# A decoder layer's prologue: first scores by halves of the keys, chunk 1 between the first steps, other load order, idle matmuls

## The chip, the cores and the metric

The kernel runs on one core of one Trainium2 chip. The metric is the time of one execution in device microseconds (us), taken as the median over runs; lower is better. A core has five engines that work at the same time, each through its own instructions in order, and that wait for each other by semaphores: TensorE (PE, matrix products; its weight loads are listed apart as PEld), VectorE (DVE), ScalarE (ACT), GpSimd (POOL) and SyncE (SP), which here only issues transfers (DMAs). ACT issues some DMAs as well: such an issue stands in ACT's instruction order, and the transfer itself runs on the core's DMA engines. TensorE writes into PSUM, which has eight banks of 128 x 512 floats; DVE and ACT read results from there.

## The reference

One pre-norm decoder layer on x of shape (2, 1024, 256): self-attention, cross-attention to a context of 77 tokens, and a mixture of experts. All data are float32. The change touches only the beginning of the self-attention:

```python
x = x + _L0_attn_ref(_layernorm(x), Wq, Wk, Wv, rel_table, gamma, beta)
x = x + _L0_xattn_ref(_layernorm(x), ctx, ctx, mask, ...)
x = x + _L0_ffn_ref(_layernorm(x), ...)          # top 2 of 8 experts

def _L0_attn_ref(x, ...):                        # 16 heads of 16 channels
    q, k, v = (split_heads(x @ W) for W in (Wq, Wk, Wv))
    attn = softmax(einsum('bhqd,bhkd->bhqk', q, k) * e ** -0.5)
    attn = attn + rel_table[rel_index].reshape(h, s, s)[None]
    out = layernorm(merge_heads(einsum('bhqk,bhkd->bhqd', attn, v)), eps=1e-3)
    return out * gamma + beta
```

## The kernel before

The 2048 tokens lie in `xs` as 16 tiles of 128 rows; four tiles make a *chunk* (512 tokens), so chunks 0 and 1 are batch 0, and 2 and 3 are batch 1. The work of a chunk before attention is a chain of small helpers:

- `load_x(c)` (L98) loads the chunk from HBM by SP. `load_rows` (L105) loads a weight matrix, by ACT for Wk and Wq and by SP for Wv.
- `measure(c)` (L159, L160): mean and variance of each token, two DVE instructions a tile. `deviation(c)` (L136, L137): the variance plus epsilon on DVE, then to the power of -0.5 on POOL, whose second operand is the constant tile `nhalf`.
- `scale_tokens(0)` (L316) normalises chunk 0 on DVE. For other chunks `offsets(c)` (L172, DVE) and `scale(c)` (L183, four ACT instructions) do it.
- `turned(c, kc, copy)` (L193, L196): four transposes on TensorE into one PSUM bank, then one copy into `xnT`, by DVE or by ACT. There are two such halves `kc` of 128 channels.
- `project(w, name, j)` (L495): K or Q of 512 tokens for eight heads, two matmuls. Q is copied by ACT (L505). K is written twice by DVE (L510), once for each of two groups of heads, as `kT0` and `kT1`.
- `values(c, u)` (L333, L340): V of two tiles, four matmuls and an ACT copy into `vaug`. `clear(kt)` (L296, L297) fills the rest of `vaug` on POOL, `clear_rest` other tiles.

Wk and Wq lie in HBM in another order of heads than the projections need, so ACT rearranges them first, by four copies each (L279), out of `wkraw` and `wqraw`.

Attention is one stream of 128 steps (`for n in range(steps + 1)`), eight steps for each of 16 *halves* (a batch, a group of four heads, 512 queries). In step n, `stream_a` (L525) computes four score tiles of 128 queries by 512 keys, one for each head, and DVE takes the maximum of each row (L532). Two steps make one tile of 128 queries, since there are 1024 keys. Eight steps give the maxima of a half. `find_shift` (L540), `shift_queries` (L551, L554: four transposes into the tile `pm`, then one DVE instruction) turn them into an extra channel of the queries. Ten steps behind (`LAG = 10`), `stream_b` (L571) computes the scores again with keys in rows, already shifted; ACT takes their exponentials (L579), and `times_v` (L588) multiplies by V.

The order on TensorE, DVE, ACT and POOL is the order in which the program is written (`manual_schedule`); SP's instructions are ordered by the framework. `between` is a table of jobs that are written ahead of step n. In the kernel before, chunks 0 and 1 are measured, scaled and turned, and K of batch 0's first eight heads is projected for both, before step 0; the values of chunks 0 and 1, and chunks 2 and 3, follow in steps 0 to 8, the context's keys and values in steps 7 to 9. The loads are written at the head, from L245 on; the ACT ones (Wk, Wq) are the first instructions of ACT, ahead of its table load.

Of the kernel before, what the change touches and what calls it, by code (L numbers as in the profile page):

```python
# [11 lines left out]
ALU = mybir.AluOpType  # L12
AX = mybir.AxisListType

P = 128
# [25 lines left out]
def decoder_kernel(  # L41
# [55 lines left out]
    def load_x(c):  # L97
        nc.sync.dma_start(  # L98
            out=xs[:, 4 * c : 4 * c + 4, :],
            in_=xf[512 * c : 512 * c + 512, :].rearrange("(t p) d -> p t d", p=P),  # L100
        )
# [60 lines left out]
    def deviation(c, eps=1e-5):  # L162

        tokens[c] = norm_scale(moments[c][1], 4, eps)
# [78 lines left out]
    make_identity(nc, ident)  # L243
    nc.gpsimd.memset(nhalf, -0.5)
    load_x(0)  # L245
    for name, src in (("wk", a_wk), ("wq", a_wq)):
        raws[name] = load_rows(src, f"{name}raw", D, fst)
    load_x(1)
# [19 lines left out]
    nc.vector.tensor_reduce(  # L268
        hsel, ident.rearrange("p (a j r) -> p j a r", a=2, j=4), AX.XY, ALU.add
    )  # L270
    nc.scalar.mul(hsel, hsel, 0.25)
    for name, raw in raws.items():
        c0 = {"wk": 2048, "wq": 2560}[name]
        w = scrap[:, c0 : c0 + 512].rearrange(
# [17 lines left out]
    def clear(kt):  # L292

        part = vaug[:, kt : kt + 2]
        for k in range(2):
            nc.gpsimd.memset(part[:, k, :, DH:, :], 0.0)  # L296
            nc.gpsimd.memset(part[:, k, :, DH, :], 1.0)  # L297
# [188 lines left out]
    units = {}  # L486
    outs = {}

    def project(w, name, j):

        b, G = w // 2, w % 2
        cols = slice(512 * j, 512 * j + 512)
        pp = one("pp")
        for kc in range(2):
            nc.tensor.matmul(  # L495
                pp,
                lhsT=wqk[name][:, kc, P * G : P * G + P],
                rhs=xnT[:, kc, b * S + 512 * j : b * S + 512 * j + 512],
                start=(kc == 0),
                stop=(kc == 1),  # L500
            )
        if name == "wq":
            if j == 0:
                units[w, "q"] = scrap[:, 3584 + S * (w % 2) : 3584 + S * (w % 2) + S]
            nc.scalar.copy(units[w, "q"][:, cols], pp)  # L505
            return
        for i in range(2):
            if j == 0:
                units[w, "k", i] = at2.tile([P, S], F32, tag=f"kT{i}", name=f"kT{i}_{w}")
            nc.vector.tensor_scalar(  # L510
                units[w, "k", i][:, cols], pp, own[i][:, 0:1], extra[i][:, 0:1], ALU.mult, ALU.add
            )

    pieces = [("wk", 0), ("wq", 0), ("wk", 1), ("wq", 1)]
    largest = {}

    def stream_a(n, hh):
        h, r = n // 8, n % 8
        b, g, qb = halves[h]
        if h not in largest:  # L520
            largest[h] = at2.tile([P, 4, 4, 2], F32, tag="mx", name=f"mx{h}", bufs=3)
        qt, kh = r // 2, r % 2
        s = one("sA")
        r0, q0 = 32 * hh, 512 * qb + P * qt
        nc.tensor.matmul(  # L525
# [359 lines left out]
    def shared(c, u):  # L885

        psh = one("psh").rearrange("p (t f) -> p t f", f=D)
        for t in range(2):
# [12 lines left out]
    turns = [("a", 0), ("b", 1), ("a", 2), ("b", 3), ("b", 0), ("a", 1), ("b", 2), ("a", 3)]  # L901


    between = {
        0: [lambda: values(0, 0), lambda: measure(2)],
        1: [lambda: values(0, 1), lambda: deviation(2), lambda: clear(0)],
        2: [lambda: values(1, 0), lambda: project(0, "wq", 1), lambda: offsets(2), lambda: clear(2)],
        3: [lambda: values(1, 1), lambda: scale(2), lambda: measure(3), lambda: clear(4)],
        4: [
            lambda: turned(2, 0, by_act), lambda: turned(2, 1, by_act), lambda: deviation(3),  # L910
            lambda: clear(6), rest_of_loads,
        ],
        5: [lambda: values(2, 0), lambda: offsets(3), lambda: scale(3), clear_rest],
        6: [lambda: values(2, 1), lambda: turned(3, 0, by_act), lambda: turned(3, 1, by_act)],
        7: [lambda: values(3, 0), context_turn, lambda: context_keys(0)],
        8: [lambda: values(3, 1), lambda: context_keys(1), mask_bias],
# [11 lines left out]
    between.update({40 + 4 * c: [lambda c=c: add_rows(c, beta_a)] for c in range(4)})  # L928
    measure(0)
    deviation(0)  # L930
    measure(1)
    deviation(1)
    scale_tokens(0)
    turned(0, 0, by_dve)
    turned(0, 1, by_act)
    offsets(1)
    scale(1)
    project(0, "wk", 0)
    project(0, "wq", 0)
    turned(1, 0, by_dve)  # L940
    turned(1, 1, by_act)
    project(0, "wk", 1)

    def settle(c, n):

        key = "o", c
# [631 lines left out]
```

## Time and profile before

| | |
|---|---|
| median of 3 runs (lowest, highest) | 1005.02 us (1004.63, 1005.73) |
| the profiled execution | 1004.62 us, span 1002.9 us |
| mean granted TensorE clock | 0.956 |
| attention's stream of steps | from 24 us (first scores) to about 510 us |
| cross-attention and routing | to about 670 us |
| mixture of experts | to about 956 us, then the last sums and norms |
| first token load landed, DVE starts on it | 6.04 us |
| first instruction of TensorE | 11.24 us |
| first exponential of the stream | 60.13 us |

The span reaches from the first instruction of the program to its last; the time of the execution holds 1.7 us more. In a line of the timeline the first number is the start in us from the span's start, the second the length, then the engine, the source line, the operation, output and inputs, shapes and the number of instructions merged; in brackets stands the engine's idle time before it and what ended that. A float32 matrix product is recorded as two rows of TensorE, a transpose as one. In a line of the table of stretches, the first pair is the stretch, then come its length, the busy time of PE, PEld, DVE, ACT and POOL (with counts), the granted clock, the busy share of the DMA engines and the GB/s that they moved.

### The profile page before, as it was taken

The numbers are of one execution on the slowest core, as the hardware profiler recorded it, in microseconds if no ns is written. First come the engines' busy times: TensorE is split into PE (matmuls) and PEld (weight loads), VectorE is DVE, ScalarE is ACT, GpSimd is POOL, SyncE is SP. The second block draws the span as 40 slices with busy tenths as digits, with TensorE's granted clock in tenths as the row PEclk, the third lists the DMA queues.
The fourth block names the chain that finished last, engine by engine and source line by source line (L and its number), as shares of the span: only waits on it lengthen the run. The fifth ranks groups of instructions, "written<-read, shape, count | busy, mean of one in ns | idle before, by whom it ended". The sixth has DMA issues, their size and how long they took to land.

```text
span 1002.9 us, 15898 instructions
## 1 busy us (share of the span) xinstructions
PE 894.6 (89%) x5948; PEld 516.9 (52%) x5948; DVE 594.9 (59%) x1185; ACT 536.1 (53%) x1064; POOL 403.9 (40%) x336
## 2 busy tenths in 40 slices
PE   5999999999999999999946999979999999998900
PEld 2543433333333333333314667767788788887800
DVE  4876658877897787987589998760110110110057
ACT  3457667777887786887844777313322222233301
POOL 1533223553335544343466887023444421222125
PEclk9999999999999999999977999998999999998955
DMA  8200000000000000000000000146645645799152
GB/s 177 50 1 1 2 2 1 2 1 1 1 1 1 1 2 1 1 1 2 1 1 18 1 22 23 42 133 230 196 163 189 207 155 174 256 318 318 65 173 84
DMA packets 65143, 75.63 MB, mean 75 GB/s; under 512 B 17947, under 2 KB 57016, under 8 KB 65056
## 3 DMA queue, kind: packets, MB, share of 16 engines
q1 hardware_dynamic: 59040, 63.09, 19.9%
q0 software_dynamic: 3360, 8.79, 2.3%
q10 hardware_dynamic: 2656, 2.62, 0.8%
q8 instruction: 50, 0.82, 0.3%
q14 instruction: 37, 0.30, 0.1%
HBM read 66.10 MB, written 8.78 MB: 75 GB/s over the span
## 4 chain that ended last, share of the span: by engine, by line
PE 53%; DVE 14%; DMA 13%; issue 11%; POOL 6%; ACT 2%; POOLq 0%; ACTq 0%; DVEq 0%; SPq 0%
PE sA L525 15%; PE av L588 12%; DMA pairs<-y,to_row 11%; PE sB L571 11%; PE pp L495 3%; POOL pairs L1452 2%; PE pv L333 2%; DVE scrap L1516 2%; PE pb L387 1%; DVE cm L676 1%; PE ph L1422 1%; POOL xg L1396 1%; DVE cs L688 1%; PE pq L640 1%; DVE scrap L672 1%
## 5 line engine op out<-in xcount | busy, mean ns | idle before, releaser
L532 DVE TENSOR_REDUCE mx<-sA 128x1 f32<-128x512 f32 x512 | 317.5, 683 | 71.5 <-PE sB L571 63.8
L579 ACT ACTIVATE pt<-sB 128x512 f32<-128x512 f32 x512 | 264.6, 603 | 79.8 <-PE sB L571 79.6
L525 PE MATMUL sA<-kT,scrap 32*128 32x512 f32 x1024 | 259.2, 619 | 0.0
L601 POOL TENSOR_TENSOR avs<-avs,part 128x512 f32<-128x512 f32 x112 | 142.1, 1268 | 269.9 <-ACT part L600 264.6
L571 PE MATMUL sB<-qB,kT 32*128 32x512 f32 x1024 | 248.5, 616 | 0.0
L1429 ACT ACTIVATE hT<-ph,b1s 128x256 f32<-128x256 f32 (+1 forms) x184 | 77.8, 424 | 186.5 <-PE ph L1422 184.4
L525 PEld LDWEIGHTS sA<-kT,scrap 32*128 32x128 f32 x1024 | 101.5, 183 | 87.8 <-ACT pt L579 52.3
L1441 PE MATMUL po<-w,hT 128*128 128x256 f32 x560 | 139.2, 387 | 6.5 <-DVE y L1448 5.2
L1422 PE MATMUL ph<-xgT,w 128*128 128x256 f32 (+1 forms) x736 | 139.6, 336 | 2.0 <-ACT hT L1429 2.0
L588 PE MATMUL av<-pt,vaug 128*32 128x512 f32 x1024 | 137.4, 605 | 1.7 <-DVE mx L532 1.7
L1422 PEld LDWEIGHTS ph<-xgT,w 128*128 128x128 f32 x736 | 117.5, 193 | 26.7 <-ACT hT L1429 11.3
L1448 DVE TENSOR_TENSOR y<-po,b 128x512 f32<-128x512 f32 (+1 forms) x23 | 13.0, 564 | 187.1 <-PE po L1441 180.4
L571 PEld LDWEIGHTS sB<-qB,kT 32*128 32x128 f32 x1024 | 97.7, 183 | 38.4 <-issue 30.1
L1441 PEld LDWEIGHTS po<-w,hT 128*128 128x128 f32 x560 | 101.5, 192 | 21.3 <-DVE y L1448 8.3
L1452 POOL DMA_INDIRECT pairs<-y,to_row x35 | 35.5, 1016 | 123.9 <-DMA pairs<-y,to_row 82.5
L1396 POOL DMA_INDIRECT xg<-xnd,from_row x35 | 34.2, 976 | 100.0 <-PE px L1412 61.9
L588 PEld LDWEIGHTS av<-pt,vaug 128*32 128x32 f32 x1024 | 21.0, 109 | 98.8 <-DVE mx L532 85.3
L600 ACT COPY part<-av 128x512 f32<-128x512 f32 x108 | 65.6, 608 | 8.1 <-PE av L588 7.9
L137 POOL TENSOR_TENSOR rstd<-rstd,nhalf 128x4 f32<-128x4 f32 x20 | 21.7, 1086 | 68.3 <-DVE rstd L136 68.2
L193 PE MATMUL pxT<-ident,xn 128*128 128x128 f32 x96 | 18.2, 309 | 28.8 <-ACT xn L183 17.4
L495 PE MATMUL pp<-xnT,scrap 128*128 128x512 f32 x64 | 33.3, 648 | 0.4 <-DVE xnT L196 0.3
L705 ACT COPY PT<-ppT 77x512 f32<-77x512 f32 x64 | 32.4, 588 | 2.0 <-DVE xs L1052 1.0
(239 smaller groups left out, 958.3 us busy)
## 6 DMA issues: line engine op xcount, KB each, us to landing
w<-in_L_ffn_W_dram SPq DMA_DIRECT2D x46, 1024.0 KB, 7.4
b<-in_L_ffn_b_dram SPq DMA_DIRECT2D x23, 128.0 KB, 6.6
xs<-in_x_dram SPq DMA_DIRECT2D x4, 512.0 KB, 8.2
xnd<-xn SPq DMA_DIRECT2D x4, 512.0 KB, 2.9
w<-pairs SPq DMA_DIRECT2D x4, 512.0 KB, 9.4
w<-pairs ACTq DMA_DIRECT2D x4, 512.0 KB, 7.4
out_dram<-scrap SPq DMA_DIRECT2D x4, 512.0 KB, 2.9
mk<-in_mask_BxSxS_ik_dram SPq DMA_DIRECT2D x1, 616.0 KB, 6.0
```

What stands on the lines that cost most here:

```text
L495: nc.tensor.matmul(pp, lhsT=wqk[name][:, kc, P * G : P * G + P], rhs=xnT[:, kc, b * S + 512 * j : b * S + 512 * j + 512], start=(kc == 0), ...
L525: nc.tensor.matmul(s, lhsT=units[h // 4, "q"][r0 : r0 + 32, q0 : q0 + P], rhs=units[h // 4, "k", g % 2][r0 : r0 + 32, 512 * kh : 512 * kh ...
L532: nc.vector.tensor_reduce(largest[h][:, qt, hh : hh + 1, kh], s, AX.X, ALU.max)
L571: nc.tensor.matmul(s, lhsT=units[h // 4, "k", g % 2][r0 : r0 + 32, kt * P : (kt + 1) * P], rhs=shifted[h][r0 : r0 + 32, :], start=True, st ...
L579: nc.scalar.activation(powers[m, hh], s, AF.Exp, scale=1.0 / 16.0)
L588: nc.tensor.matmul(av[32 * hh : 32 * hh + 32, :], lhsT=vaug[:, kt, 4 * g + hh, :, b], rhs=powers.pop((m, hh)), start=True, stop=True,)
L600: copy(part, av)
L601: nc.gpsimd.tensor_tensor(sums[h], sums[h], part, ALU.add)
L1422: nc.tensor.matmul(ph[:, hc % group, :], lhsT=w1[:, kc, hc * P : (hc + 1) * P], rhs=xgT[:, kc, :], start=(kc == 0), stop=(kc == 1),)
L1429: hidden[i] = nc.scalar.activation(hT[:, hc, :], ph[:, hc % group, :], AF.Gelu, bias=b1s[:, i, hc : hc + 1])
L1441: nc.tensor.matmul(po[:, s, :], lhsT=hT[:, hc, s * P : (s + 1) * P], rhs=w2[:, hc, :], start=(hc == 0), stop=(hc == NH - 1),)
L1452: nc.gpsimd.indirect_dma_start(out=pairs[:, :], out_offset=bass.IndirectOffsetOnAxis(ap=to_row[:, k : k + 1], axis=0), in_=y[:, s, :], in_ ...
```

## The change

1. **Loads.** An ACT instruction that multiplies one column of `nhalf` by 1.0 is written ahead of the loads of Wk and Wq; it waits for POOL's fill of `nhalf`, and it brings ACT's table load with it. The scaling of `hsel` by 0.25 goes from ACT to DVE.
2. **Idle matmuls.** 22 products of the identity matrix with itself go to a PSUM bank that nobody reads, as the first work of TensorE.
3. **Order of scores.** In the first half (n < 8), step n takes tile n % 4 of the queries and half n // 4 of the keys, so that steps 0 to 3 use keys 0 to 511 alone.
4. **Chunk 1 between the steps.** Half of chunk 1's statistics are written behind chunk 0's scaling. Its `offsets` and `scale` go into `between[0]`, its `turned` into `between[1]`, K's second projection into `between[2]` and Q's into `between[3]`. The values, chunk 2's and the clearing are redistributed: values (0, 0) and (0, 1) go from steps 0 and 1 to 2 and 3, values (1, 0) and (1, 1) from 2 and 3 to 4 and 5, behind chunk 2's transposes and ahead of values (2, 0).
5. **Second copy of the keys.** `project` can put off the write of `kT1`, which the first group of heads doesn't use; it is done one step later.

```diff
     load_x(0)
+    nc.scalar.mul(nhalf[:, 0:1], nhalf[:, 0:1], 1.0)
+    idle = one("idle")
+    for _ in range(22):
+        nc.tensor.matmul(idle[:, :P], lhsT=ident, rhs=ident, start=True, stop=True)
     for name, src in (("wk", a_wk), ("wq", a_wq)):
         raws[name] = load_rows(src, f"{name}raw", D, fst)
...
-    nc.scalar.mul(hsel, hsel, 0.25)
+    nc.vector.tensor_scalar(hsel, hsel, 0.25, None, ALU.mult)
...
-    def project(w, name, j):
+    def project(w, name, j, put_off=None):
...
-        for i in range(2):
+        def keys(i):
             if j == 0:
                 units[w, "k", i] = at2.tile([P, S], F32, tag=f"kT{i}", name=f"kT{i}_{w}")
             nc.vector.tensor_scalar(
                 units[w, "k", i][:, cols], pp, own[i][:, 0:1], extra[i][:, 0:1], ALU.mult, ALU.add
             )
+        keys(0)
+        if put_off is None:
+            keys(1)
+        else:
+            put_off.append(lambda: keys(1))
...
-        qt, kh = r // 2, r % 2
+        qt, kh = (r % 4, r // 4) if n < 8 else (r // 2, r % 2)
...
+    keys_of_1 = []
     between = {
-        0: [lambda: values(0, 0), lambda: measure(2)],
-        1: [lambda: values(0, 1), lambda: deviation(2), lambda: clear(0)],
-        2: [lambda: values(1, 0), lambda: project(0, "wq", 1), lambda: offsets(2), lambda: clear(2)],
-        3: [lambda: values(1, 1), lambda: scale(2), lambda: measure(3), lambda: clear(4)],
+        0: [lambda: offsets(1), lambda: scale(1)],
+        1: [
+            lambda: keys_of_1.pop(0)(), lambda: turned(1, 0, by_dve), lambda: turned(1, 1, by_act),
+            lambda: clear(0), lambda: clear(2),
+        ],
+        2: [
+            lambda: project(0, "wk", 1, keys_of_1), lambda: values(0, 0), lambda: measure(2),
+            lambda: deviation(2),
+        ],
+        3: [
+            lambda: keys_of_1.pop(0)(), lambda: values(0, 1), lambda: project(0, "wq", 1),
+            lambda: offsets(2), lambda: scale(2), lambda: measure(3), lambda: clear(4),
+        ],
         4: [
             lambda: turned(2, 0, by_act), lambda: turned(2, 1, by_act), lambda: deviation(3),
-            lambda: clear(6), rest_of_loads,
+            lambda: clear(6), rest_of_loads, lambda: values(1, 0),
         ],
-        5: [lambda: values(2, 0), lambda: offsets(3), lambda: scale(3), clear_rest],
+        5: [lambda: values(1, 1), lambda: values(2, 0), lambda: offsets(3), lambda: scale(3), clear_rest],
...
     measure(0)
     deviation(0)
-    measure(1)
-    deviation(1)
+    measure(1, [0, 1])
     scale_tokens(0)
     turned(0, 0, by_dve)
     turned(0, 1, by_act)
-    offsets(1)
-    scale(1)
-    project(0, "wk", 0)
+    measure(1, [2, 3])
+    deviation(1)
+    project(0, "wk", 0, keys_of_1)
     project(0, "wq", 0)
-    turned(1, 0, by_dve)
-    turned(1, 1, by_act)
-    project(0, "wk", 1)
```

## The prediction

> **What bounds the kernel now.** I read the page's table of engines first, then its slices, then the timeline of the first 60 us by engine, what SP's queue waited for, and tables by stretch of time.
>
> ```profile
> PE 894.6 (89%) x5948; PEld 516.9 (52%) x5948; DVE 594.9 (59%) x1185; ACT 536.1 (53%) x1064; POOL 403.9 (40%) x336
> PE   5999999999999999999946999979999999998900
> ```
>
> TensorE is the bound in nearly every slice; only the first (25 us) is half empty. The diff ends before step 10 of the attention loop, where the stream of exponents starts, so it can only shift the arrival there: the first transposes of shifts ("pm", L551) begin at 57.04 us, and what follows is issued in the same order in both programs. I therefore price that one moment.
>
> ```profile
> 8.23 0.90 ACT L279 COPY scrap<-wqraw 128x128 f32<-128x128 f32 x4 [1.58 <-DMA wqraw<-in_L_attn_Wq_dram]
> 11.24 2.30 PE L193 MATMUL pxT<-ident,xn 128*128 128x128 f32 x8 [11.24 <-DVE xn L316]
> 13.56 5.82 PE L495 MATMUL pp<-xnT,scrap 128*128 128x512 f32 x8
> 17.11 0.34 PEld L495 LDWEIGHTS pp<-xnT,scrap 128*128 128x128 f32 x1 [0.52 <-issue]
> 17.93 0.19 PEld L495 LDWEIGHTS pp<-xnT,scrap 128*128 128x128 f32 x1 [0.49 <-issue]
> 20.60 1.98 PE L495 MATMUL pp<-xnT,scrap 128*128 128x512 f32 x4 [0.35 <-DVE xnT L196]
> 35.53 2.07 ACT L183 ACTIVATE xn<-xs,off,rstd 128x256 f32<-128x256 f32 x4
> 58.73 7.27 DVE L532 TENSOR_REDUCE mx<-sA 128x1 f32<-128x512 f32 x12 [0.23 <-PE sA L525]
> ```
>
> PE waits 11.24 us for chunk 0's normalised tokens, then runs almost without a gap. Up to 17.9 us its weight loads take 0.34 us and its matmul rows come every 0.85 us; from 17.93 on 0.19 and 0.43. That is the clock: half until there, full after, although the granted clock reads 1.00 in both stretches (it is recorded only from its first change on).
>
> ```profile
> SPq L253 <- DMA xs<-in_x_dram: 2.2, 2, 1.1
> SPq L253 <- DMA wqraw<-in_L_attn_Wq_dram: 1.7, 1, 1.7
> 7.00:8.40 1.40, 0.00 (x0) 0.00 (x0) 1.27 (x6) 0.17 (x1) 0.00 (x0) 1.00 1.10 348
> ```
>
> SP's small loads wait for the landing of loads they have nothing to do with: DMAs share eight semaphores in turn, and the ninth waits until the first has landed. The transfers together move 350 KB/us.
>
> **Part by part.** *Loads.* Wk and Wq leave the ACT queue behind one ACT operation, so semaphores are dealt anew. In the changed program's order x takes the first, second, fourth and fifth, wv the third; Wk's issue shares the second, so it waits for chunk 1's landing, and Wq's shares the fourth and waits for chunk 2's. Before, both went at 0.80 and 1.32. By the table of stretches (76 KB/us from 1.75 to 2.75, 96 to 3.25, 217 to 3.75, 362 to 4.25, 385 to 5.25, 377 to 6.00) 1081 KB had gone by 6.00 us, then 350 KB/us; a load's last share lands 1.0 us after its bytes are counted (chunk 1: 1573 KB at 7.4, landed 1.30+7.1=8.4). So chunk 1 (1049 KB in) lands at 6.9; chunk 2 has 1835 KB up to its end, with Wk's 262 up to 2097: 8.2 to 8.9, landed 9.2 to 9.9, I take 9.3. A 256 KB load alone: 512 KB went out in 2.9, less 256/350=0.73, is 2.2; cwu's 256 KB among others took 3.6. I take 2.7, as SP's queue is nearly drained by then (all of x at 10.5). Wq lands at Q=12.0, bounds 11.3 and 13.5. Before: 8.2. SP's own small loads change their waits too, but the first use of any (cx, by PE) is at 48 us, twenty us after the last of SP's issues here.
>
> ACT works in order: Wq's copies (0.90) and only then chunk 0's second xnT copy (0.59). So the projections go on at P = 12.0+0.90+0.59+0.06 = 13.55. **That chunk 0 lands early gains nothing**: with its 524 KB alone from the start it lands between 5.1 (510 KB had gone by 4.5, plus 0.6) and 6.0 as before; its scaling began 4.74 after landing and now 1.05 less (two of chunk 1's statistics go behind it), the first transpose 0.46 later: 9.25 to 10.15. Transposes end near 11 and their copy stands behind Wq on ACT. The Wq wait is the new one; queued behind it on ACT are that copy, q's copy and chunk 1's scaling.
>
> *Idle matmuls.* 22 matmuls of 128x128 are 44 rows. The eight of "pin" (16 rows) took 2.03 us at full clock: 0.12 a row, so 5.3 us warm, 10.5 cold. They start when ident is ready (1.4). Cut every 3.41 us (17.89, 516.24, 536.71, 543.54), stretches read 0.50 or 1.00 throughout, so the clock steps at such edges, and it turns somewhere between 4.9 and 8.3 us and the idle work ends between 8.3 and 10.0, before or about when the first transposes are due (9.3); P hides them all. If the clock never turned they would end at 11.9, still before P.
>
> *Sum on TensorE, from 13.56 to 57.04 = 43.48 us before.* Of this the half clock costs (17.9-13.56)/2 = 2.2. Stalls: 0.35 for xnT (row above), 1.35 at chunk 2's transposes (from the end of scores at 36.08 to the next at 38.35 is 2.27, the eight transposes need 0.92), 0.73 at the context keys: 2.43. Bare work: 38.85. After, from P: bare work less the first half of K's projection, done while Wq is awaited (two rows, 0.86): 37.99. New stalls, laid out with the same rows: projections end at 13.55+0.86+1.72=16.13; q's copy (0.59) and two hand-overs let scores start at 16.80: stall 0.67 (before, chunk 1's transposes stood there). Scores 1.07, to 17.87. Chunk 1's scaling follows q's copy on ACT, 16.75 to 18.82, so the eight transposes end at 19.44, not 18.79: 0.64. Scores of step 1 to 20.51. K's projection of chunk 1 needs DVE: four mx (2.45) from 17.12, the put-off keys 0.77, the xnT copy 0.69, to 21.03: 0.56. Then 1.72, values 1.86, scores, values, projection, scores: to 30.40. Chunk 2's offsets come out of DVE at 29.99 (mx, key, statistics ahead of them), its scaling takes to 32.10, the transposes end at 32.72: 1.40, as before. Context keys 0.67. Total 3.94. So pm at 13.55+37.99+3.94 = 55.48, **1.56 us earlier**: +0.01 start, 0.86 overlap, 2.2 clock, -1.51 stalls.
>
> Scores in two key halves add no row: the first four steps use keys 0-511 and chunk 0's queries only, so chunk 1's work may stand behind them. DVE's extra hsel product (about 0.16, as the neighbouring small operations) hides in its 3.57 us wait for x; ACT's table load (1.28) moves under the first loads. DVE stays behind PE by little: its 7.27 us run of mx at 58.73 follows pm in both, so the shift carries through. POOL's clears move earlier into 16 us of idleness.
>
> Before's profiled execution took 1004.62 (span 1002.9 and 1.7 around it); less 1.56 is 1003.06. The median of the runs is 1005.02, 0.40 higher, so I forecast **1003.4**. By the bounds of Q alone each us is a us: 1002.7 to 1004.9.
>
> [...] The step down is in the trace:
>
> ```profile
> 540.12:543.54 3.42, 0.81 (x6) 0.59 (x6) 3.28 (x13) 0.70 (x2) 2.25 (x1) 1.00 0.36 117
> 543.54:546.95 3.41, 3.41 (x16) 2.59 (x14) 3.38 (x7) 0.00 (x0) 1.40 (x1) 0.50 0.00 0
> 618.63:622.04 3.41, 2.32 (x20) 1.85 (x17) 2.62 (x7) 3.41 (x7) 0.86 (x1) 1.00 0.43 154
> ```
>
> (length, then PE, PEld, DVE, ACT, POOL busy, granted clock, DMA.) A stretch with 0.81 us of work ends at half clock; one with 2.32, of which 2.13 are transposes, does not. In the new order the stretch between the idle work and the projections holds eight transposes (0.92) and two rows (0.86), with gaps: between those rows, nearer the second, if the stretch begins when both fall in it.
>
> [...]
>
> **Rivals.**
> *Forecast, 0.36:* clock holds, Q near 12. 1003.4, own range 1002.8 to 1004.3. For: the two rows above; against: it needs transposes to count.
> *Faster, 0.38:* Wq lands about 11.0 (a lone load without cwu's company, chunk 2 not slowed by Wk), the clock turned early: 1003.4-1.0 = 1002.4. For: SP's first load moves alone. Against: ACT's copies still stand behind Wq.
> *No gain, 0.14:* the clock falls for one stretch of 3.41 us (P to 17.0): about 2.0 of the 2.2 is given back, or the idle work doesn't raise it. The change then warms nothing it was to warm: 1005.2.
> *Slower, 0.12:* the clock falls between idle work and projections and stays down two stretches, 14.3 to 21.1. Warm work under it (projections 2.58, scores 1.07) doubles: +3.65, less 0.67 of stall that it covers; with Q at 13.1 another 1.1: 1003.4+3.0+1.1 = 1007.5. For: one full low stretch suffices (540.12), and a late Wq makes one. Against: two low ones in a row are needed. It decides from about 3.6 us lost.
>
> **How the numbers follow.** About 0.2% (2.0 us) is what a measurement of this kernel can tell from no change: faster is below 1003.0, slower above 1007.0. The forecast lies just inside "same"; together with no gain that makes 0.50, faster 0.38, slower 0.12. The range 1002.0 to 1006.0 reaches below Q's early bound by the runs' own spread (0.5) and to the no-gain case; the slower case is left out.
>
> **What would show it.** Right: Wq's copies begin near 12 and Wk's near 10, each load issued just after chunk 2 and chunk 1 landed; ACT's second xnT copy right behind; K's second row near 13.6 with weight loads of 0.19; pm near 55.5. Wrong: Wq's copies before 11 or after 13.5; 0.34 us weight loads after 12 us; first transposes held by the idle rows past 10.5; or a DVE wait in steps 1 to 4 longer than 1.5 us that lets PE's gain run out. I would be wholly wrong if the times differ after pm, for instance at the end of attention, by something other than the shift there.

## The result, and the profile after

| | before | after |
|---|---|---|
| median of 20 runs each (lowest, highest) | 1005.50 us (1001.89, 1007.52) | 1004.22 us (998.18, 1012.03) |
| ratio, 95% interval | | 1.0002 (0.9979 to 1.0026) |
| the profiled execution | 1004.62 us, span 1002.9 | 1000.20 us, span 998.5 |
| first transposes of shifts ("pm") | 57.04 us | 55.43 us (forecast 55.48) |
| TensorE's last instruction | 952.6 us | 948.8 us |

The median was forecast at 1003.4, with no difference as the likeliest class. It came at 1004.2, and the interval of the ratio holds 1, so no difference is shown. (The ratio is the comparison's own; that of the two medians is 0.9987.) Two things were not foreseen: the profiled execution gained 4.4 us and not 1.6, and seven of the 20 runs lie together at 1010 to 1012, with a mean granted clock of 0.946 to 0.948, where the other thirteen lie below 1005 at 0.950 to 0.961. The seven are called the *far runs* below, the others the near group; in the other comparisons a far run is one above 1009.

First the page of the changed kernel: busy time by engine, and TensorE's slices of 25 us.

```profile
PE 900.1 (90%) x5992; PEld 523.8 (52%) x5992; DVE 595.0 (60%) x1186; ACT 535.8 (54%) x1064; POOL 403.3 (40%) x336
PE   7999999999999999999946999988999999999900
```

The 44 more instructions are the idle rows; the first slice went from 5 to 7 tenths with them. TensorE's timeline of the changed kernel:

```profile
1.43 7.31 PE L251 MATMUL idle<-ident 128*128 128x128 f32 x44 [1.43 <-POOL nhalf L244]
9.14 1.74 PE L193 MATMUL pxT<-ident,xn 128*128 128x128 f32 x8 [0.40 <-DVE xn L322]
11.76 1.13 PE L501 MATMUL pp<-xnT,scrap 128*128 128x512 f32 x2 [0.89 <-ACT scrap L285]
13.64 2.84 PE L501 MATMUL pp<-xnT,scrap 128*128 128x512 f32 x6 [0.75 <-ACT xnT L196]
17.16 1.14 PE L539 MATMUL sA<-kT,scrap 32*128 32x512 f32 x8 [0.68 <-ACT scrap L511]
...
22.17 1.98 PE L501 MATMUL pp<-xnT,scrap 128*128 128x512 f32 x4 [0.79 <-DVE xnT L196]
...
55.43 0.60 PE L565 MATMUL pm<-ident,shift 128*128 128x128 f32 x4
```

The idle rows end at 8.74 and the transposes start 2.1 us earlier than before (9.14 for 11.24), but the projections go on at 13.64, no earlier than before (13.56): the wait behind "ACT scrap" and "ACT xnT" is the one for the weights. The gain of 1.6 us appears between there and 55.43, where TensorE now runs at full clock from the first projection (its weight loads behind 13.64 take 0.19 us; before's took 0.34 up to 17.9). ACT's timeline, with its DMA issues, shows the wait from the other side:

```profile
6.52 0.42 ACTq L105 DMA_DIRECT2D wkraw<-in_L_attn_Wk_dram  x1
8.83 0.38 ACTq L105 DMA_DIRECT2D wqraw<-in_L_attn_Wq_dram  x1
11.41 0.90 ACT L285 COPY scrap<-wkraw 128x128 f32<-128x128 f32 x4 [9.11 <-DMA wqraw<-in_L_attn_Wq_dram]
12.21 0.89 ACT L285 COPY scrap<-wqraw 128x128 f32<-128x128 f32 x4
13.01 0.57 ACT L196 COPY xnT<-pxT 128x512 f32<-128x512 f32 x1
```

Wk is issued right after chunk 1 landed (6.50 in the trace's semaphore events), Wq after chunk 2 (8.81). Wk's first packet moves only at 9.03, as SP's earlier loads run dry (their queue moves 84 KB in the quarter of a microsecond up to 9.0, 64 and 24 KB in the next two), so both weights land late, Wk at 11.39 and Wq at 11.76, and both sets of copies stand in a row ahead of the second xnT copy. (The first bracket names wqraw, but the copies that it stands at need Wk alone, and Wk's landing is what they follow.)

Behind "pm" the shift carries through attention unchanged: the last product of attention starts at 514.16 instead of 515.71 (-1.55), the gate's product of chunk 1 (the routing's narrow product with `fgw`, L755 before and L769 after) at 620.63 instead of 622.21 (-1.58). The first experts' transpose comes at 675.97 instead of 677.24 (-1.27), the experts take 272.8 us instead of 275.3, and what follows TensorE's last instruction 49.7 instead of 50.3. So of the profiled 4.4 us the prologue gave 1.6, of which 0.3 is lost again behind the gate; most of the rest (2.5) came in the experts, which the change doesn't touch.

### The profile page after: what moved, and what is told of

The parts are those of the page before. It is cut to its first block, busy times and chain, and to the rows that moved or that the text cites. A ratio compares the mean times of both kernels' runs of the same rounds, so it can differ in the third digit from the quotient of the medians.

```text
span 998.5 us, 15985 instructions
## 1 busy us (share of the span) xinstructions
PE 900.1 (90%) x5992; PEld 523.8 (52%) x5992; DVE 595.0 (60%) x1186; ACT 535.8 (54%) x1064; POOL 403.3 (40%) x336
## 4 chain that ended last, share of the span: by engine, by line
PE 69%; DVE 15%; DMA 9%; ACT 2%; POOL 2%; issue 2%; SPq 0%; POOLq 0%; ACTq 0%; DVEq 0%
PE sA L539 15%; PE av L602 12%; PE sB L585 11%; PE ph L1441 9%; PE po L1460 9%; DMA pairs<-y,to_row 7%; PE pp L501 3%; DVE scrap L1535 2%; PE pb L393 1%; PE pv L339 1%; DVE cm L690 1%; DVE cs L702 1%; PE pq L654 1%; DVE scrap L686 1%; DVE mx L546 1%
## 5 line engine op out<-in xcount | busy, mean ns | idle before, releaser
L1471 POOL DMA_INDIRECT pairs<-y,to_row x35 | 35.1, 1003 | 118.2 <-DMA pairs<-y,to_row 81.4
```

What stands on the lines that cost most here:

```text
L1471: nc.gpsimd.indirect_dma_start(out=pairs[:, :], out_offset=bass.IndirectOffsetOnAxis(ap=to_row[:, k : k + 1], axis=0), in_=y[:, s, :], in_ ...
```

## The experiments

"The changed kernel" and "before" name the two kernels of the case. Each was compared with before on the same chip, but not all on one chip, so that medians of different rows compare only roughly; the ratio is the safer column. Eleven other kernels ran, and the changed kernel once more:

| run | median (lowest to highest), runs | before there | ratio (95%) | "pm" |
|---|---|---|---|---|
| no idle matmuls | 1006.99 (1003.01 to 1015.34), 12 | 1005.85 | 1.0004 (0.9981 to 1.0027) | 55.66 |
| weights issued first | 1003.87 (999.14 to 1013.50), 12 | 1005.85 | 0.9996 (0.9963 to 1.0030) | 54.86 |
| before + 22 idle | 1002.38 (999.34 to 1010.88), 12 | 1005.85 | 0.9969 (0.9946 to 0.9991) | 55.51 |
| weights on SP's queue | 1002.86 (999.83 to 1012.67), 12 | 1005.85 | 0.9964 (0.9935 to 0.9993) | 55.74 |
| changed + gate filled | 1001.70 (999.08 to 1004.18), 12 | 1005.84 | 0.9955 (0.9932 to 0.9978) | 56.30 |
| changed kernel again | 1004.85 (998.90 to 1011.52), 12 | 1005.84 | 0.9992 (0.9966 to 1.0018) | 56.16 |
| before + 32 idle | 1000.60 (996.89 to 1003.79), 12 | 1005.84 | 0.9942 (0.9922 to 0.9962) | 54.48 |
| SP weights, all filled | 999.93 (996.98 to 1000.88), 9 | 1005.84 | 0.9937 (0.9913 to 0.9961) | 54.80 |
| before + gate filled | 1001.95 (1000.30 to 1002.46), 6 | 1005.78 | 0.9966 (0.9953 to 0.9979) | 56.47 |
| before, all filled | 998.76 (997.16 to 1001.61), 6 | 1005.78 | 0.9939 (0.9924 to 0.9955) | 54.55 |
| before, all filled, SP weights | 1001.44 (996.70 to 1010.65), 12 | 1005.78 | 0.9971 (0.9941 to 1.0000) | 54.35 |
| changed, all filled | 999.90 (999.56 to 1000.34), 5 | 1006.30 | 0.9937 (0.9924 to 0.9951) | 55.39 |

### What each part of the prologue is worth

**The changed kernel without its idle matmuls.**

```diff
-    idle = one("idle")
-    for _ in range(22):
-        nc.tensor.matmul(idle[:, :P], lhsT=ident, rhs=ident, start=True, stop=True)
```

> The changed kernel without the 22 idle matmuls, all else as it is. Main theory (the prologue's gain is the clock of the first work plus the overlap, less the new stalls, and the shift at the first transposes of shifts goes through to the end): the projections go on at 13.6 us as before, but at half clock until somewhere between 16 and 19 us; bare work between 13.6 and there costs double, so the first transposes of shifts begin 1.0 to 2.5 us later than 55.4, at 56.4 to 57.9, and the profiled prologue is within 0.9 us of the kernel before (57.04). Runs spread as widely as the changed kernel's (998 to 1012), because the far runs come from the clock's later falls. Rival (the idle work itself makes the far runs near 1011 us, by where it puts the clock's edges): the spread shrinks to that of before (1002 to 1007.5) and no run lies above 1009. Rival (the clock is worth nothing there, PE waits anyway): 55.4 as with the idle work.

TensorE's timeline of this run:

```profile
9.37 2.30 PE L193 MATMUL pxT<-ident,xn 128*128 128x128 f32 x8 [9.37 <-DVE xn L319]
12.01 4.72 PE L498 MATMUL pp<-xnT,scrap 128*128 128x512 f32 x8 [0.34 <-ACT scrap L282]
...
55.66 0.60 PE L562 MATMUL pm<-ident,shift 128*128 128x128 f32 x4
```

A miss: 55.66, earlier than the 56.4 to 57.9 expected. In this execution the clock turned full at 13.71, when the projections had only just gone on. In the records of before and of the changed kernel, all eleven later changes of the granted clock lie a whole number of stretches of 3.41 us behind the first (17.89 and 5.94). Such edges lay differently against the program in these profiles: the clock turned at 13.71 here, and at 17.89 and 17.12 in the two profiles of before's own prologue. So the idle rows' 2.2 us are the price of one execution's edge; here they were worth 0.23. One of the twelve runs lay above 1009 (1015.34), so the far runs need no idle matmuls. The runs don't follow "pm": it comes 1.38 us earlier than in before, and yet the ratio to before is 1.0004. The run of before with five idle matmuls at the gate, further down, comes back to this.

**The changed kernel with Wk and Wq issued before the ACT operation.**

```diff
-    nc.scalar.mul(nhalf[:, 0:1], nhalf[:, 0:1], 1.0)
...
     for name, src in (("wk", a_wk), ("wq", a_wq)):
         raws[name] = load_rows(src, f"{name}raw", D, fst)
+    nc.scalar.mul(nhalf[:, 0:1], nhalf[:, 0:1], 1.0)
```

> The changed kernel with the ACT operation (L247) moved behind the two weight loads, so that Wk and Wq are issued at the start and wait for no landing, as before the change. Main theory (the weights' late landing sets when the projections go on; chunk 0 landing early alone gains nothing): x lands at 6.0 instead of 5.0, first transposes at 10.2 instead of 9.1, but the copies of Wk and Wq are done by 9.2, so the second xnT copy follows the transposes at once; projections go on near 12.5 instead of 13.64, less 0.5 to 0.9 of overlap lost; first transposes of shifts at 54.6 to 55.4, so up to 0.8 us earlier than the changed kernel. Rival (chunk 0 alone is what pays): 1.0 us later, near 56.4.

```profile
10.07 1.73 PE L193 MATMUL pxT<-ident,xn 128*128 128x128 f32 x8 [0.97 <-DVE xn L322]
12.25 3.67 PE L501 MATMUL pp<-xnT,scrap 128*128 128x512 f32 x8 [0.44 <-DVE xnT L196]
...
54.86 0.60 PE L565 MATMUL pm<-ident,shift 128*128 128x128 f32 x4
```

DVE starts on chunk 0 at 5.96 instead of 5.02 and the transposes come 0.9 us later, yet all eight rows of the projections follow from 12.25 without a break and "pm" comes 0.57 us earlier than in the changed kernel. With the clock held in both, 0.57 is the price of the new load order in these two profiles. The rival (chunk 0 alone is what pays) falls.

**Before, with idle matmuls and nothing else**, 22 in one run and 32 in another.

```diff
+    idle = one("idle")
+    for _ in range(22):   # 32 in the second
+        nc.tensor.matmul(idle[:, :P], lhsT=ident, rhs=ident, start=True, stop=True)
     for name, src in (("wk", a_wk), ("wq", a_wq)):
```

> The kernel before with nothing but the 22 idle matmuls added. Main theory: the clock is full from some point between 5 and 8 us; the idle rows end near 8.7, the first transposes come at 11.2 as before; if the clock holds over the 2.5 us between, the transposes, projections and scores of the first 18 us run at full clock: 1.1 us at the transposes and 2.2 behind them at most, of which the later stalls on DVE and ACT take back a part; first transposes of shifts at 53.8 to 55.4, that is as early as in the whole change or earlier: the idle work is then nearly all of the change's gain. If the clock falls in the gap: 55.5 to 56.5. Rival (the new order and the loads carry the gain): 56.5 to 57.0, hardly moved.

> The kernel before with 32 idle matmuls and nothing else, so that the idle rows end between 10.4 and 11.5 us and meet the first transposes (11.3). With 22 the idle rows ended at 8.07 and the clock fell for the stretch 11.35 to 14.76, and yet the first transposes of shifts came at 55.51. Theory: held at full, the transposes take 1.1 us less than 2.30 or the time of their inputs, and the projections up to 14.76 0.6 us less: first transposes of shifts at 53.9 to 55.0, so the idle work alone does as much as the whole change (55.43), and order and loads add nothing to it. Rival (order and loads carry a part, because stalls on DVE and ACT come back in the old order): 55.4 or later.

TensorE's timeline of before with 32:

```profile
1.43 8.82 PE L248 MATMUL idle<-ident 128*128 128x128 f32 x64 [1.43 <-POOL nhalf L244]
10.97 1.73 PE L193 MATMUL pxT<-ident,xn 128*128 128x128 f32 x8 [0.72 <-DVE xn L319]
13.14 3.67 PE L498 MATMUL pp<-xnT,scrap 128*128 128x512 f32 x8 [0.44 <-DVE off L172]
...
54.48 0.60 PE L554 MATMUL pm<-ident,shift 128*128 128x128 f32 x4
```

With 22 the idle rows end at 8.1, TensorE waits 3.2 us, and the clock is down from 11.35 to 14.76; "pm" is at 55.51 all the same. With 32 they reach to 10.25, the clock holds (the eight rows of the projections take 3.67 us, 4.24 with 22), and "pm" is at 54.48: 0.95 us earlier than the whole change with a held clock (55.43). So by these profiles the idle work alone gains more in the prologue than the whole change (from 57.04, or 56.47 in the second profile of before's own prologue, to 54.48). Order and loads together take 0.95 back, of which 0.57 are the loads (run above) and 0.38, by difference, the order and the smaller number of idle matmuls. The median with 32 gains 5.2 us, twice the 2.6 of "pm", so about half of it isn't the prologue's.

**The changed kernel with the weights on SP's queue behind chunk 0**, and chunk 1's statistics behind chunk 0's scaling.

```diff
-        raws[name] = load_rows(src, f"{name}raw", D, fst)
+        raws[name] = load_rows(src, f"{name}raw", D, fst, nc.sync)
...
-    measure(1, [0, 1])
     scale_tokens(0)
     turned(0, 0, by_dve)
     turned(0, 1, by_act)
-    measure(1, [2, 3])
+    measure(1)
```

> The changed kernel with Wk and Wq issued from SP's queue between chunk 0 and chunk 1 (no issue waits for a landing, chunk 0 still lands alone), and all of chunk 1's statistics behind the scaling of chunk 0. Main theory: chunk 0 lands at 5.0 to 5.5, Wk and Wq by 7.5, their copies are done by 9; the second xnT copy follows the transposes at 10.9, projections go on at 11.6 instead of 13.64; chunk 1 lands near 8.4, early enough. First transposes of shifts at 53.2 to 54.6, about 1 to 2 us earlier than the changed kernel. Rival (DVE and chunk 2, not the weights, set the first steps): stalls grow by as much and it stays at 55.0 to 55.6.

The projections started at 11.43 as expected, but the clock fell from 11.42 to 14.83 in this execution and they took 5.36 us instead of 3.67; "pm" came at 55.74, a miss. Its span was 1010.3, a far run with a profile, and that led on.

### Where the far runs come from

**The changed kernel once more**, for another profile beside the next run.

> The changed kernel as it is, beside the others on this chip. Theory: the prologue's gain is one to two us, and the runs fall into the same groups as before (998 to 1005, and about 1010 to 1012 in up to a third of them), so the median is 1002.5 to 1005 and the median of the near group is 2 to 3 us below that of the kernel before. Its own profile shows the first transposes of shifts at 55.4 if the clock holds up to the projections, up to 57.1 if a stretch falls. Rival (the far group of the first 20 runs was an accident of one chip): no run above 1008.

The runs came as expected (1004.85, three of twelve above 1009 against two of 32 of before on that chip), and the profiled execution is a far one, with a span of 1009.8. Its table of stretches, cut at the edges of the clock:

```profile
8.30:11.72 3.42, 1.74 (x8) 0.94 (x8) 2.82 (x9) 0.27 (x2) 0.27 (x1) 1.00 0.83 261
11.72:15.13 3.41, 3.33 (x4) 1.34 (x5) 0.59 (x3) 1.90 (x9) 2.56 (x6) 0.50 0.63 90
619.29:622.70 3.41, 2.15 (x19) 1.87 (x18) 3.10 (x11) 3.41 (x9) 2.27 (x2) 1.00 0.16 54
622.70:626.11 3.41, 3.41 (x18) 3.41 (x18) 2.06 (x10) 1.65 (x4) 0.98 (x1) 0.50 0.00 0
629.52:632.94 3.42, 3.42 (x20) 0.79 (x16) 0.00 (x0) 0.58 (x1) 0.00 (x0) 0.50 0.00 0
639.76:643.18 3.42, 3.42 (x9) 2.70 (x9) 1.69 (x5) 0.00 (x0) 0.00 (x0) 0.50 0.02 5
```

The first stretch holds the eight transposes and no other work of TensorE (1.74 of 3.42 us), and the clock falls for the next (0.50): the one-stretch fall of the prediction's third case ("no gain"). "pm" comes at 56.16 instead of 55.43, so it costs 0.73. At 622.70 the clock falls again and stays at half for six stretches, 20.48 us, although TensorE reads busy all the time (for the whole 3.41 or 3.42 us of each). Its work there is the gate's products (128x8), transposes, products of 77x512 (with weights of 77*32), small products of 128x8 to 128x64, and at the end products of 128x256, with their weight loads. The stretch from 629.52 holds products of 77x512 alone, one behind the other, and the clock stays down; which work counts how much is not settled here. The stage from the gate's product of chunk 1 to the first expert takes 66.5 us, 11 more than in the first profile: 9.9 more up to the gate's product of chunk 2 (25.1 for 15.2), and 1.6 more from there to that of chunk 3, where the clock falls once more, for one stretch from 650.0. That is the far run. The same two places in the first profile of the changed kernel, where the edges lay 1.05 us otherwise:

```profile
9.35:12.77 3.42, 2.53 (x10) 1.10 (x9) 2.58 (x9) 1.36 (x7) 0.24 (x1) 1.00 0.57 152
616.92:620.33 3.41, 2.46 (x21) 2.00 (x19) 2.48 (x6) 3.41 (x7) 0.72 (x1) 1.00 0.44 153
```

Here the transposes share their stretch with K's first two rows (2.53 us busy of 3.42), the wait of 1.26 us at the gate is split between two stretches (2.46 of 3.41 us busy in the first), and the clock holds at both (1.00). Put side by side from all profiles with the old gate (an edge of the clock less the start of the gate's product; time at half clock that follows this edge; from the product to the first expert):

```
changed kernel       -0.3 us    0       55.3 us
before               -0.2       0       55.0
no idle              +0.4       0       55.0
weights issued first +1.1       6.83    59.5
changed, again       +1.4      20.48    66.5
weights on SP        +1.4      20.48    66.6
before + 22 idle     +1.6       3.41    56.7
before + 32 idle     +1.9       3.41    56.7
```

The instructions at the gate are the same in all these rows; only the edge's place differs. In the rows with an edge 1.1 to 1.9 us behind the product, one stretch holds the wait, the narrow product and little else (2.15 of 3.41 us busy in the changed kernel again, 2.16 of 3.42 in before + 22 idle), and the clock fell in each. The rows with 6.83 and 20.48 have one more fall, of 3.41, behind the gate's product of chunk 2.

**The changed kernel with five idle matmuls in that wait.**

```diff
+    def keep_busy(n):
+        bank = one("idle")
+        for _ in range(n):
+            nc.tensor.matmul(bank[:, :P], lhsT=ident, rhs=ident, start=True, stop=True)
     work_of = dict(
+        idle=keep_busy,
...
-        sums:15 shares:15 stats:2:1 flip:1:1:0 stats:2:0 flip:1:0:0 turn:14 dev:2 gate:1
+        sums:15 shares:15 stats:2:1 flip:1:1:0 stats:2:0 flip:1:0:0 turn:14 dev:2 idle:5 gate:1
```

> The changed kernel with five more idle matmuls before the gate's product of chunk 1 (L769), where TensorE waits 1.26 us for xnT at 619.4 us. [...] With the gap filled no stretch there falls under 0.40: no run above 1008, spread 998 to 1005, median 0.5 to 2 us below the changed kernel's 1004.2; the mean granted clock is 0.950 or more in every run. Rival (the far runs come from somewhere else, or the gap is not what decides): 3 or 4 of 12 runs still lie at 1010 to 1013 with a clock of 0.945 to 0.948.

No run above 1004.2, as expected, and 1001.7 in the median, 3.2 below the changed kernel on the same chip (0.5 to 2 below 1004.2 had been expected). No run shows the 0.40 of the expectation; what the profiles show is busy time and the place of the edges, which lay 1.7 us apart against the product in the first profile of the changed kernel and in that with the weights on SP's queue, by the rows above. This profile has an edge at 623.07, 1.6 us behind the product, and yet:

```profile
619.65:623.07 3.42, 3.36 (x30) 3.12 (x28) 2.91 (x11) 3.42 (x8) 2.47 (x2) 1.00 0.09 30
```

TensorE is busy 3.36 us of that stretch instead of 2.15, and the clock holds where it fell in the five rows with such an edge. So the long fall comes from that wait. Twelve runs alone would be thin evidence, against three far ones in twelve; the profile is what decides. Not all falls are gone: behind the gate's product of chunk 2 the clock is down from 640.13 for one stretch, and the stage takes 56.7 us here. In the prologue it fell for one stretch too (12.08 to 15.50; "pm" 56.30, 0.87 late).

**Before, with the same five in the same place.**

> The kernel before with nothing but five idle matmuls ahead of the gate's product of chunk 1. Theory: the far group goes here too (2 of 32 runs of before lay above 1013 in the last comparison, 11 of 32 runs of the changed kernel above 1009), but the prologue stays at 56 to 57, so the near group stays where it is: 1001.5 to 1008.5, median 0 to 1 us below before. The 4 us between before and the changed kernel with the filled gate are then mostly the prologue and the runs that the change had lost at the gate. Rival (the filled gate alone makes those 4 us): median near 1002.

Here the theory failed and the rival's number came: 1001.95. But the profile doesn't give it to the gate. The edge lay 0.35 us ahead of the product, where the unfilled kernels hold too (-0.3 to +0.4 in the rows above), and from the gate to the experts it took 55.0 us, as in before. Nor is it the clock: five runs of before on that chip with a granted clock of 0.955 to 0.957 have a mean of 1004.1, four of this kernel with 0.956 or 0.957 one of 1001.4. Of the 4.3 us between the two profiles' spans, 0.6 lie in the prologue, 2.1 in the experts and 1.6 behind TensorE's last instruction. In the experts, before has this in TensorE's timeline:

```profile
922.93 1.23 PE L1422 MATMUL ph<-xgT,w 128*128 128x128 f32 x4
925.36 3.78 PE L1441 MATMUL po<-w,hT 128*128 128x256 f32 x8 [1.20 <-issue]
```

and the changed kernel without idle matmuls, the only other one with before's 5948 TensorE rows, has a like one there:

```profile
922.09 0.60 PE L1438 MATMUL ph<-xgT,w 128*128 128x128 f32 x3
924.49 0.27 PE L1438 MATMUL ph<-xgT,w 128*128 128x128 f32 x1 [1.80 <-issue]
```

"issue" is time in which TensorE waited for nothing that the profile shows; a packet of the instruction queue moves at 922.8 in the one and 921.8 in the other, while the weights load. The twelve profiles of other row counts have no wait over 0.9 us there; seven of them have one near 884 to 890 instead. The experts take 275.3 and 275.6 us in these two, and 271.0 to 273.6 in the others but one (before filled, with the weights on SP's queue: 277.2, with a wait of 3.78). So by the profiles some 2 us in the experts go with having no idle rows at all, in two kernels of different order and loads, and are not seen in 11 of the 12 profiles with idle rows; comparisons with before may hold them. That the position of the instruction loads makes them, and that any added rows move it, fits all this, but was not tried by itself: no run adds rows where they can do nothing else.

### With every long wait filled

Three versions got idle matmuls in the other waits in which the clock fell: before with 32 at the start; the same with 24 there, the weights on SP's queue and chunk 1's statistics behind chunk 0's scaling; and the changed kernel with its own 22. The last two also have one behind each of chunk 0's first three transposes and two or three ahead of the first projection. The part that they share:

```diff
-        less:1 scores:2 masked:2 o_add:14 times_v:127:0 less:0 collect:15 exps:1
+        less:1 scores:2 masked:2 o_add:14 times_v:127:0 less:0 idle:17 collect:15 idle:70 exps:1
...
-        sums:15 shares:15 stats:2:1 flip:1:1:0 stats:2:0 flip:1:0:0 turn:14 dev:2 gate:1
+        sums:15 shares:15 stats:2:1 flip:1:1:0 stats:2:0 flip:1:0:0 turn:14 dev:2 idle:5 gate:1
...
-        filled:3 pick shared:2:1 rows biases shared:1:0
+        filled:3 pick shared:2:1 rows biases shared:1:0 idle:18
```

> The kernel before with 32 idle matmuls at the start, 17 and 70 around the last product of the attention, 5 ahead of the gate of chunk 1 and 18 ahead of the experts; order and loads as before. With the 32 alone the first transposes of shifts came at 54.48 and the median at 1000.6. Theory: the clock holds through the wait of 15 us at 515 (54 rows' worth were 3.7 us too few, and the clock fell at 529.8), so the context scores start warm: 1 to 2 us there, 1 to 1.5 at the experts' first tile; 997 to 1000, no run above 1003. Rival (DVE and the gather's DMA set the end of those stages): 999.5 to 1001, as with the 32 alone.

> As the filled version of the kernel before, with Wk and Wq on SP's queue behind chunk 0, 24 idle matmuls at the start, one behind each of the first three transposes and two behind the last, and chunk 1's statistics behind chunk 0's scaling. Theory: the first transposes at 9.3 to 10 instead of 10.97, projections near 11.5 to 12.2 instead of 13.14; chunk 1's scaling on ACT ends near 15.5 and costs up to 0.7 of stall: first transposes of shifts at 53.0 to 54.2, 0.3 to 1.5 us below 54.48. Rival (chunk 1's statistics and scaling, not the weights, hold the second transposes): 54.5 to 55.3, nothing gained.

> The changed kernel, its order and loads as they are, with the later idle matmuls of the filled version of the kernel before (17 and 70 around the last product of the attention, 5 at the gate, 18 ahead of the experts), and in the prologue one behind each of the first three transposes and three before the first projection, so that the clock holds until the projections. It stands against the filled version of the kernel before, which has the old order and loads, a held clock, first transposes of shifts at 54.55 and a median of 998.8. Theory (with the clock held, the late weights and the new order cost about 0.9 us): first transposes of shifts at 55.3 to 55.8, median 999.3 to 1000.8. Rival (the new order and the early chunk have something to give once nothing disturbs the clock): 54.5 or earlier and 998.8 or less.

An earlier version of this, on the changed kernel with the weights on SP, had 13 and 54 instead of 17 and 70; those ended at 526.3 and the clock fell at 529.84.

> The changed kernel with the weights on SP's queue (first transposes of shifts at 55.74 with the clock fallen from 11.42 to 14.83), and idle matmuls wherever TensorE waits long and the clock fell in the profiles: 25 at the start, one behind each of the first three transposes and two behind the last, 13 and 54 around the last product of the attention (waits of 3.8 and 15.3 us), 5 ahead of the fifth context scores, 5 ahead of the gate of chunk 1, 14 ahead of the experts (4 us). Theory (each fall costs about half of the warm work under it, and shows only where TensorE is the bound): prologue 1.7 us earlier (first transposes of shifts at 53.5 to 54.6), 1 to 2.5 us between 530 and 546, 1 to 2 us at 676 to 683, and no far runs: 994 to 1000, mean granted clock 0.97 or more. Rival (those stretches are bound by DVE, ACT and DMA, and the idle rows stand in the way): 1000 to 1004.

It came at 999.93, at the slow end of the 994 to 1000 expected. "pm" missed, 54.80 for 53.5 to 54.6, and so did the clock, 0.965 to 0.969 for 0.97 or more. Its 25 idle matmuls met a late edge (7.60) and ended at 10.2, so that the first transpose came at 10.04, where the same loads without the fill had 9.25. Before filled has the lowest median of all, 998.76, with no run above 1003, as expected; but by the ratio to before on its own chip the three best filled versions (0.9937 to 0.9939) can't be told from each other, nor from the 32 alone (0.9942). The wait at 515 in its table of stretches, then in before's:

```profile
514.50:530.00 15.50, 15.34 (x136) 14.96 (x134) 15.05 (x32) 3.46 (x4) 8.42 (x6) 1.00 0.00 1
```

```profile
514.50:532.00 17.50, 0.66 (x4) 0.42 (x4) 17.05 (x34) 4.17 (x5) 10.90 (x7) 0.55 0.00 0
```

The clock is full there instead of half (1.00 for 0.55 over the stretch), but the stage is bound by DVE (15.05 of 15.50 busy): from the last product of attention to the gate's product it took 106.6 us with the fill and 106.5 without: the fill gained nothing there, as the rival had it. What its profile has less than that of the 32 alone lies in part between the gate and the experts (55.2 us against 56.7) and in the experts (271.3 against 273.6). The changed kernel, filled, came at 999.90 with "pm" at 55.39, both as expected. That is 0.84 us behind before filled at "pm": with the clock held in both, its order and its loads cost about that much of the prologue. The medians lie 1.1 us apart, but on different chips, and the ratios (0.9937 and 0.9939) show no difference. The third version, 54.35 at "pm" (53.0 to 54.2 expected), is unclear: four of its twelve runs lie at 1007 to 1011 with a clock of 0.958 to 0.960, two of them above 1009 although the wait at the gate is filled, and its profile has a wait of 3.78 us at 883.9 in the experts with the clock down behind it. That wasn't followed up.

## Why the prediction was right, and where it failed

**The load chain** was right in its sum and wrong in one link. The issues waited for chunk 1 and chunk 2 as told (6.52 and 8.83; 6.9 and 9.3 had been taken). Wq landed at 11.76 for 12.0. Wk, whose copies had been put near 10, landed at 11.39: its first packet moved at 9.03, when SP's earlier loads were running dry, and that it waited for them is read from this alone. So both copies stood ahead of the second xnT copy, Wq's began at 12.21, and the projections went on at 13.64 for 13.55. That chunk 0's early landing gains nothing as long as the weights come late is borne out by the run with the weights issued first: chunk 0 a microsecond later, and "pm" 0.57 earlier. The faster rival, Wq at about 11.0, didn't come.

**Clock, overlap and stalls.** From 13.64 to 55.43 are 41.79 us; 41.93 were told. Against the stalls of the prediction (in brackets): q's copy 0.68 (0.67); chunk 1's transposes, from the end of scores at 18.23 to the next at 19.82 less 0.92 of work, 0.67 (0.64); the wait for DVE's xnT copy 0.79 (0.56); chunk 2's transposes, from the end of scores at 31.59 to the values at 33.84 less 0.92, 1.33 (1.40); the context keys 0.74 (0.67). That makes 4.21 for 3.94, and leaves 37.58 of bare work for 37.99. "pm" missed its number by 0.05 us, but in part because these two errors cancel. It was luck too that the profiled execution held its clock: two other profiles of the same prologue didn't.

**The third case was too dear and too rare.** A fall of one stretch between idle work and projections, given a chance of 0.14, happened in two of the three profiles of the changed prologue. It costs 0.73 and 0.87, not the 2.0 of the prediction. That took the stretch to begin when the projections go on; it begins at 11.7 to 12.1, so that a good part of it covers K's first half, which waits anyway. From 13.64 to 15.13, at half clock, it can cost (15.13-13.64)/2 = 0.75. The slower case (two stretches) was not seen.

**The step that failed** is "what follows is issued in the same order in both programs. I therefore price that one moment". The order is the same and attention keeps the shift to 0.1 us. But the granted clock changed only at edges 3.41 us apart, which lay between 0.3 us ahead of the gate's product and 1.9 behind it in the eight profiles with the old gate, and what came after differed with their place: by 11 us behind the gate alone (55.3 and 66.5 us in two profiles of the changed kernel). Over all comparisons, 10 of 32 runs of the changed kernel (not 11, as one expectation has it) and 6 of 113 of before lie above 1009. In both far runs that were profiled (of the changed kernel and of the one with the weights on SP's queue) the time is lost in the fall behind the gate, and the filled wait takes that fall away; the other far runs have no profile. Why the changed kernel meets it more often is open, since before with 22 idle matmuls has the same shift at attention's end and one far run in twelve. And the profiled 4.4 us held 2.5 from the experts, where the prediction had put none: by its own last sign, times that differ after "pm", it was wrong there. The median came near the forecast because these two went against each other, which is luck, and not only because the prologue was told well. The 0.5 us that its range allowed for the runs' spread came from three runs; the 20 of before span 5.6 us and those of the changed kernel 13.9.

**Transposes and the clock.** The prediction took transposes to count as work. The row from 618.63 held the clock with mostly transposes (2.13 of its 2.32 us busy); the changed kernel has a stretch of transposes alone, at half clock:

```profile
535.00:538.41 3.41, 3.41 (x17) 3.41 (x17) 3.41 (x3) 1.65 (x3) 1.44 (x1) 0.50 0.04 1
```

It holds transposes of "pxT" and "ppT" and nothing else, 3.41 of 3.41 us, and at its end (538.41) the granted clock rose from 0.50 to 1.00. By these two rows they count in these float32 kernels. The edges lay differently in two executions of the changed kernel (the first at 5.94 and at 4.89 us), and the prediction should have carried that to the end of the program.

## What to carry to other kernels

Price a shift at the program's start where it lands last: here a stage whose TensorE work is thin lost several times the gain when the clock's edges fell otherwise (11 us against 1.6), and one profile shows one position of the edges only. Idle matmuls can pay in a wait behind which TensorE is the bound, if they leave little of it: in before, 32 at the start ended 0.72 us ahead of the transposes, the clock held and "pm" came at 54.48; 22 ended 3.22 us ahead, the clock was down from 11.35 to 14.76 and "pm" came at 55.51. Where DVE was the bound (15.05 of 15.50 us busy) they gained nothing (106.6 us for 106.5). Before a small gain in a median is put down to a change, try the same number of added rows where they can do nothing else: here some 2 us in the experts may have come with any rows added. Before a load is written later, look which landing its semaphore will make it wait for, and what queue of packets stands ahead of it: here Wk was issued at 6.52, behind chunk 1's landing at 6.50, and its first packet moved at 9.03.

## What the runs showed that was not expected

- TensorE read busy all through six stretches (the whole 3.41 or 3.42 us of each, 20.48 in all) while the granted clock stayed at 0.50, so the busy time in the record doesn't tell by itself when the clock rises. One of the six is full of products of 77x512 alone.
- With five idle matmuls in a wait of 1.26 us, none of 12 runs lay in the group some 8 us above the others (they lay at 999.1 to 1004.2), where 10 of 32 did without them.
- A load of 256 KB, issued at 6.52, moved its first packet at 9.03 on a second queue while the first still had work, and landed with the one issued 2.3 us later.
